# Folding the attention weights of layer 1 at the end of layer 0, and reading them back from DRAM

## The chip, the cores and the metric

The kernel is one program on one core of a Trainium2 chip. The metric is device time in microseconds (us). Times of whole runs are given as a median of several; a profiled execution has its own time, and within it the span from the first instruction to the last.

## What is computed

Two layers run one after the other on x of shape 4 x 512 x 512, all in float32. Layer 0 is a test-time-training scan (32 heads of 16, 32 steps of 16 tokens) beside a gated feed-forward network of width 1408. Layer 1 is a latent attention (16 heads of 128, four batches of 512 tokens here seen as 4 x 512 rows) beside four experts of width 512. Cut to what matters:

```python
xn = layernorm(x)
x = x + ttt_scan(xn) @ o_w.T + ffn(xn)                 # layer 0
xn = layernorm(x)
c_kv = xn @ W_DKV + b_DKV                              # latents, 128 wide
c_q  = xn @ W_DQ + b_DQ                                # latents, 384 wide
k = (c_kv @ W_UK + b_UK).reshape(b, s, H, D)           # H = 16, D = 128
v = (c_kv @ W_UV + b_UV).reshape(b, s, H, D)
q = (c_q @ W_UQ + b_UQ).reshape(b, s, H, D)
q[..., :64] = rope(q @ W_QR); k[..., :64] = rope(k @ W_KR)
probs = softmax(q . k / sqrt(D))
x = x + (probs @ v).reshape(b, s, H * D) @ W_O + b_O + experts(xn)   # layer 1
```

Two products of weights alone can be taken ahead of the tokens. The rotated half of a key or query is c @ (W_U @ W_R), so W_U @ W_R (64 columns per head) is one folded weight; and probs @ v @ W_O is (probs @ c_kv) @ (W_UV @ W_O), so W_UV @ W_O (512 columns per head) is another. What b_UV adds to the output is one row, b_UV @ W_O, which goes into the output bias.

## The kernel before, in words

The program has three stages, each with its own pools.

**Layer 0** (lines 89 to 799). The scan runs 32 steps in eight chunks of four. A step is a chain of small operations over all engines. Between its parts `fill(us)` takes pieces of other work out of one generator, `work`, until the costs that the pieces yield (an estimate of TensorE time) cover the gap: `GAPS` for the steps of chunks 0 to 6, `LAST_GAPS` for those of chunk 7. `work` is `between(ch)` for each chunk: the feed-forward network of the chunk (`gate_up`, `down`), the next chunk's keys, values and queries, the end of the chunk before (`finish`), and in chunks 1 to 4 `value_bias`, which puts b_UV @ W_O of one group of four heads into `bo` by matmuls. `between(7)` also computes the latents c_kv and c_q of chunks 0 to 6 (`latents`) and puts them into DRAM (`lat_d`). After the last step, lines 794 to 799 take `finish(7)` apart by `LAST_FINISH`, then drain `work`, the rest of `finish(7)` and `latents(7)`.

**Experts** (lines 821 to 922). Four experts, each 8 groups of four matmuls 128x512 for gate and up (line 855) and 16 for down (line 900). Their loads go out on SyncE's queue (`fetch`, line 831), but for the first gate weight and 14 parts of the input, which go out on GpSimd's.

**Attention** (lines 928 to 1112). 64 units (group of four heads, batch, head). Each unit has queries and keys (lines 992, 999), scores (1008), softmax (1010 to 1015), probabilities turned by VectorE in 32x32 blocks (1023) and 16 DMAs from SBUF to SBUF (1046), context (1054); after four heads the output (1069). `group_weights` prepares a group: for group 0 ahead of the units, for groups 1 to 3 at the second batch of the group before. It loads W_UK, W_UQ, W_UV and W_O of the group, turns 128x128 blocks by TensorE (937) and ScalarE (939), and multiplies: 16 products of 64 columns (955, copied at 956) and four of 512 (970, copied at 971).

The order of the instructions on each engine is fixed when the program is built, by a scheduler, and each engine runs its own in that order; a DMA is issued by an engine's queue, in order too. The scratch tiles of layer 0 rotate by tag: `wg` and `wu` two buffers each, `wd` four, `sg` and `xr` two each. A tile of a later stage that lies where an earlier one lay waits for the last use of that one.

Of the kernel before, what the change touches and what calls it, by code (L numbers as in the profile page):

```python
# [12 lines left out]
F32 = mybir.dt.float32  # L13
AF = mybir.ActivationFunctionType
ALU = mybir.AluOpType
AX = mybir.AxisListType
PSUM = bass.MemoryType.PSUM

P = 128
B, L, HS = 4, 512, 512  # L20
NT = B * L
NC = HS // P
# [8 lines left out]
NCHUNK = NM // CH  # L31
CW = B * CT
# [1 line left out]
RW = 2 * 64 + 4  # L34

START = 20.0
GAPS, LAST_GAPS = (11.0, 4.0, 8.0), (10.0, 4.0, 5.0)
LAST_FINISH = (9.0, 17.0, 5.0)
TTT_EPS = 1e-6
LN_EPS = 1e-5  # L40

# [3 lines left out]
H, D, KVC, QC, RD = 16, 128, 128, 384, 64  # L45
HALF = RD // 2
THETA = 10000.0
NHG = 4
HPG = H // NHG
# [6 lines left out]
def trunk_kernel(ctx: ExitStack, tc: tile.TileContext, a: dict, out: bass.AP):  # L56
    nc = tc.nc
# [8 lines left out]
    ident = const.tile([P, P], F32, tag="ident", name="ident")  # L66
# [3 lines left out]
    dram = ctx.enter_context(tc.tile_pool(name="dram", bufs=1, space=bass.MemoryType.DRAM))  # L70
    yd = dram.tile([B, L, HS], F32, tag="yd", name="yd")
    xe_d = dram.tile([2 * NCHUNK, P, NC, E, 32], F32, tag="xe_d", name="xe_d")
    lat_d = dram.tile([1 + QC // P, P, B, NCHUNK, CT], F32, tag="lat_d", name="lat_d")
    bo = const.tile([P, HS], F32, tag="bo", name="bo")
    eps_ttt = const.tile([P, 1], F32, tag="eps_ttt", name="eps_ttt")
# [13 lines left out]
    with ExitStack() as px:  # L89
        one = px.enter_context(tc.tile_pool(name="b_one", bufs=1))  # L90
        wk = px.enter_context(tc.tile_pool(name="b_wk", bufs=2))
        ps_pj = px.enter_context(tc.tile_pool(name="b_pspj", bufs=2, space=PSUM))
# [4 lines left out]
        quarters = [slice(32 * q, 32 * q + 32) for q in range(4)]  # L97

        def mm(out, lhsT, rhs, start=True, stop=True):
            nc.tensor.matmul(out, lhsT=lhsT, rhs=rhs, start=start, stop=stop, skip_group_check=True)  # L100

        def psum():
            return ps_pj.tile([P, 512], F32, tag="pj", name="pj")
# [55 lines left out]
        for name in ("gamma", "beta"):  # L159
            nc.scalar.dma_start(  # L160
                out=row[name].rearrange("o (be al x) -> o be al x", be=NC, al=4),
                in_=by_head(name).rearrange("al be h d -> be al (h d)").unsqueeze(0),
# [349 lines left out]
            yield 3.43  # L512


        ones32 = one.tile([P, P], F32, tag="ones32", name="ones32")
        nc.vector.memset(ones32, 1.0 / 32)
        buv16 = one.tile([H, D], F32, tag="buv16", name="buv16")
        nc.gpsimd.dma_start(out=buv16, in_=a["b_UV"].rearrange("(h d) -> h d", d=D))
        buv_b = one.tile([P, H, 32], F32, tag="buv_b", name="buv_b")
        nc.gpsimd.dma_start(out=bo, in_=a["b_O"].unsqueeze(0).to_broadcast([P, HS]))  # L520

        def value_bias(hg):
            if hg == 0:
                pt = psum()[:, :H]
                nc.tensor.transpose(pt, buv16, ident[:H, :H])
                nc.vector.tensor_copy(buv_b, pt.unsqueeze(2).to_broadcast([P, H, 32]))
            pb = psum()
            for h, r in enumerate(quarters):
                w = wk.tile([P, HS], F32, tag="wd", name=f"wob_{hg}_{h}", bufs=4)
                nc.sync.dma_start(out=w, in_=a["W_O"][(4 * hg + h) * D : (4 * hg + h + 1) * D, :])  # L530
                mm(pb[r], buv_b[:, 4 * hg + h, :], w)
            part = wk.tile([P, HS], F32, tag="xt", name=f"bo_part{hg}", bufs=4)
            nc.vector.tensor_copy(part, pb)
            yield 1.3
            pb = psum()
            mm(pb, ones32, part)
            nc.vector.tensor_add(bo, pb, bo)
            yield 0.86

        def over_blocks(t, z):  # L540

# [108 lines left out]
        def between(ch):  # L650

            fin = finish(ch - 1) if ch > 0 else iter(())
            if ch + 1 == NCHUNK:
                latent_operands()
            for i in range(NI):
                yield from gate_up(ch, i)
                if ch + 1 == NCHUNK and i in (2, 5, 8):
                    latent_rows(i // 3)
                if i == NI - 3:
                    yield from take(fin, 1)  # L660
            if ch == 0:
                yield from finish_constants()
            extra = value_bias(ch - 1) if 1 <= ch <= NHG else iter(())
            nxt = iter(())
            if ch + 1 < NCHUNK:
                nxt = chain(
                    norm_turn(ch + 1), keys(ch + 1), token_tile(ch + 1, 0), token_tile(ch + 1, 1), queries(ch + 1)
                )
            else:
                yield from fin  # L670
            for u in range(2):
                dn = down(ch, u)
                for j in range(3):
                    yield from take(nxt, 2)
                    yield from take(dn, 1)
                    yield from take(fin, 1)
            yield from extra
            yield from nxt
            done.add(ch + 1)
            yield from fin  # L680
            if ch + 2 < NCHUNK:
                norm_rows(ch + 2)
            if ch + 1 == NCHUNK:
                for key in sorted(parts, key=str):
                    yield from latents(key)

        def take(it, k):
            for _ in range(k):
# [29 lines left out]
        pt = psum()[:, :P]  # L718
# [76 lines left out]
        for us in LAST_FINISH:  # L795
            fill(us)
            next(fin)
        for _ in chain(work, fin, latents(NCHUNK - 1)):
            pass


# [19 lines left out]
    with ExitStack() as px:  # L821
        one = px.enter_context(tc.tile_pool(name="d_one", bufs=1, reuse_waits="tile"))
        wk = px.enter_context(tc.tile_pool(name="d_wk", bufs=2, reuse_waits="tile"))
        wg = px.enter_context(tc.tile_pool(name="d_wg", bufs=1, reuse_waits="tile"))
        psp = px.enter_context(tc.tile_pool(name="d_ps", bufs=2, space=PSUM))
        gate_w = [one.tile([P, NC, 2 * EI], F32, tag="gu1", name="gu_1")]
        gate_w.insert(0, wg.tile([P, NC, 2 * EI], F32, tag="gu0", name="gu_0"))

# [40 lines left out]
        for e in range(E):  # L869
# [15 lines left out]
                    nc.sync.dma_start(out=cq[:, i], in_=lat_d[1 + i].rearrange("p b k x -> p b (k x)"))  # L885
            inter = wk.tile([P, EI // P, B * P], F32, tag="inter", name=f"inter_{e}")
            for i in range(EI // P):
                pg = psp.tile([P, B * P], F32, tag="pg", name=f"epg_{e}_{i}")
                product(e, pg, gu, i * P)
                pu = psp.tile([P, B * P], F32, tag="pu", name=f"epu_{e}_{i}")  # L890
                product(e, pu, gu, EI + i * P)
                sg = wk.tile([P, B * P], F32, tag="sg", name=f"esg_{e}_{i}")
                nc.scalar.activation(sg, pg, AF.Silu)
                nc.vector.tensor_mul(
                    by_batch(inter[:, i].rearrange("p (b j) -> p b j", b=B)), by_chunk(pu), by_chunk(sg)
                )
# [31 lines left out]
    with ExitStack() as px:  # L928
# [1 line left out]
        ps_pj = px.enter_context(tc.tile_pool(name="e_pspj", bufs=4, space=PSUM))  # L930
        ps_sc = px.enter_context(tc.tile_pool(name="e_pssc", bufs=4, space=PSUM))

        def turned(w, nm):

            pt = ps_pj.tile([P, HPG, P], F32, tag="pj", name=f"ptw_{nm}")
            for h in range(HPG):
                nc.tensor.transpose(pt[:, h, :], w[:, h, :], ident)
            t = wk.tile([P, HPG, P], F32, tag="wt", name=f"wt_{nm}")
            nc.scalar.copy(t, pt)
            return t  # L940

        def group_weights(hg):

            c = slice(hg * HPG * D, (hg + 1) * HPG * D)

            def loaded(name, src, bufs=2):
                t = wk.tile([P, HPG, src.shape[-1] // HPG], F32, tag=name, name=f"{name}_{hg}", bufs=bufs)
                nc.sync.dma_start(out=t, in_=src.rearrange("p (h d) -> p h d", h=HPG))
                return t

            def fold(w, wr, nm):
                wt = turned(w, f"{nm}_{hg}")
                pw = ps_pj.tile([P, HPG, RD], F32, tag="pj", name=f"pw_{nm}_{hg}")
                for h in range(HPG):
                    nc.tensor.matmul(pw[:, h, :], lhsT=wt[:, h, :], rhs=wr, start=True, stop=True)
                nc.scalar.copy(w[:, :, RD:], pw)

            uk = loaded("uk", a["W_UK"][:, c])
            uq = [loaded(f"uq{i}", a["W_UQ"][i * P : (i + 1) * P, c]) for i in range(QC // P)]
            uv = loaded("uv", a["W_UV"][:, c], bufs=1)  # L960
            ow = wk.tile([P, HPG, HS], F32, tag="ow", name=f"ow_{hg}", bufs=1)
            nc.sync.dma_start(out=ow, in_=a["W_O"][c, :].rearrange("(h p) o -> p h o", p=P))
            fold(uk, wkr, "uk")
            for i in range(QC // P):
                fold(uq[i], wqr, f"uq{i}")
            uvt = turned(uv, f"uv_{hg}")
            vo = wk.tile([P, HPG, HS], F32, tag="vo", name=f"vo_{hg}")
            for h in range(HPG):
                pv = ps_pj.tile([P, HS], F32, tag="pj", name=f"pvo_{hg}_{h}")
                nc.tensor.matmul(pv, lhsT=uvt[:, h, :], rhs=ow[:, h, :], start=True, stop=True)  # L970
                nc.scalar.copy(vo[:, h, :], pv)
            return dict(uk=uk, uq=uq, vo=vo)

        def rotate(t, ps, bias, trig, nm):
# [235 lines left out]
```

## Time and profile before

| what | us |
|---|---|
| median of 3 runs (lowest, highest) | 2159.91 (2157.66, 2160.46) |
| the profiled execution, whole | 2162.4 |
| its span | 2160.6 |
| first expert matmul (line 855) | 1022.40 after the start |
| first key matmul of the attention (line 992) | 1209.58 after the start |

| engine | busy us | share of the span | instructions |
|---|---|---|---|
| TensorE (PE) | 2068.6 | 96% | 10050 |
| its weight loads (PEld) | 1181.5 | 55% | 10050 |
| VectorE (DVE) | 1177.5 | 54% | 2384 |
| ScalarE (ACT) | 883.3 | 41% | 1805 |
| GpSimd (POOL) | 504.9 | 23% | 555 |

Times in the profile are us from the span's start unless marked ns. A float32 matmul of the program is two MATMUL records. SPq is SyncE's queue, whose rows are DMA issues: their durations are the time that the issue held the queue, not the transfer.

### The profile page before, as it was taken

Reading aid. Unit: us, or ns where it says so; the run is one execution under the profiler, and the core shown is the slowest. Engines: PE = TensorE matmul, PEld = TensorE weight load, DVE = VectorE, ACT = ScalarE, POOL = GpSimd, SP = SyncE. Lnnn points to the kernel's source line nnn. Section 1 sums busy time; section 2 is a strip of 40 time slices with the busy share of each in tenths; the row PEclk is TensorE's granted clock in tenths of the full one; section 3 lists DMA queues with packets and bytes.
Section 4 is the critical chain, followed back from the end, with each engine's and each line's share of the span. In section 5 each row is a group of like instructions: output and inputs, shape, how many; then the busy total and the mean of one; then the engine's idle time right before and its main releaser. Section 6 shows DMA issues by size and latency. Waiting matters only on the chain.

```text
span 2160.6 us, 29279 instructions
## 1 busy us (share of the span) xinstructions
PE 2068.6 (96%) x10050; PEld 1181.5 (55%) x10050; DVE 1177.5 (54%) x2384; ACT 883.3 (41%) x1805; POOL 504.9 (23%) x555
## 2 busy tenths in 40 slices
PE   8999999999999999995999899999999999999998
PEld 6776676767676767543444444444444444444444
DVE  4445656465656565631111556664666656666663
ACT  2334353434434343332000454444544545455552
POOL 4233233233333333301001211110111111111110
PEclk9999999999999999998999989999999999999999
DMA  6556364646474646526610233333233333333332
GB/s 179 153 138 190 112 193 134 180 135 175 131 197 129 173 136 192 171 75 235 226 59 25 89 92 77 74 94 75 76 77 93 75 72 78 75 75 75 95 94 76
DMA packets 286960, 259.27 MB, mean 120 GB/s; under 512 B 52956, under 2 KB 210845, under 8 KB 285789
## 3 DMA queue, kind: packets, MB, share of 16 engines
q1 hardware_dynamic: 272752, 245.96, 41.0%
q10 hardware_dynamic: 11500, 5.32, 0.9%
q0 software_dynamic: 2560, 6.13, 0.8%
q8 instruction: 81, 1.33, 0.3%
q14 instruction: 67, 0.54, 0.1%
HBM read 161.60 MB, written 29.62 MB: 89 GB/s over the span
## 4 chain that ended last, share of the span: by engine, by line
PE 75%; DVE 10%; ACT 9%; DMA 3%; issue 2%; POOL 1%; SPq 0%; ACTq 0%; DVEq 0%; POOLq 0%
PE pj L100 14%; PE pf L100 11%; PE po L1069 10%; PE pc L1054 7%; PE sc L1008 5%; PE pq L999 5%; PE pd L100 5%; ACT prob L1013 3%; PE epg L855 3%; PE epo L900 3%; PE epu L855 3%; ACT prob L1015 2%; PE pso L100 2%; PE pk L992 2%; PE pz L100 2%
## 5 line engine op out<-in xcount | busy, mean ns | idle before, releaser
L1008 PE MATMUL sc<-kT,qT 96*128 96x512 f32 x512 | 235.7, 598 | 15.1 <-ACT prob L1013 13.5
L985 POOL TENSOR_TENSOR kT<-t_k,t_k 32x512 f32<-32x512 f32 x64 | 80.7, 1261 | 717.9 <-PE pq L999 403.3
L1013 ACT ACTIVATE prob<-sc,mx 128x512 f32<-128x512 f32 x256 | 173.1, 683 | 147.1 <-DVE mx L1010 147.1
L1069 PE MATMUL po<-vo,ctxT 128*128 128x512 f32 x512 | 223.0, 593 | 1.5 <-ACT ctxT L1059 1.5
L1054 PE MATMUL pc<-prT,lv 128*128 128x512 f32 x496 | 224.0, 594 | 0.0
L1023 DVE STREAM_TRANSPOSE tt<-prob 128x512 f32<-128x512 f32 x252 | 166.6, 697 | 60.3 <-ACT prob L1015 56.7
L100 PE MATMUL pf<-xT,wg 128*128 128x256 f32 x704 | 171.8, 385 | 4.2 <-DVE hid L459 3.9
L999 PE MATMUL pq<-cq,uq 128*128 128x512 f32 x384 | 175.2, 592 | 0.0
L1015 ACT ACTIVATE prob<-prob,sm 128x512 f32<-128x512 f32 x256 | 171.7, 724 | 3.6 <-DVE sm L1014 3.6
L1008 PEld LDWEIGHTS sc<-kT,qT 96*128 96x128 f32 x512 | 96.0, 191 | 140.9 <-issue 110.6
L100 PE MATMUL pf<-xT,wu 128*128 128x256 f32 x704 | 168.0, 380 | 0.5 <-DMA wu<-in_wu 0.3
L1010 DVE TENSOR_REDUCE mx<-sc 128x1 f32<-128x512 f32 x256 | 164.4, 681 | 7.0 <-PE sc L1008 4.4
L100 PE MATMUL pd<-wd,hid 128*128 128x512 f32 x352 | 165.2, 600 | 0.2
L1069 PEld LDWEIGHTS po<-vo,ctxT 128*128 128x128 f32 x512 | 97.1, 190 | 124.1 <-issue 116.2
L1054 PEld LDWEIGHTS pc<-prT,lv 128*128 128x128 f32 x496 | 94.5, 191 | 120.0 <-issue 112.1
L100 PEld LDWEIGHTS pf<-xT,wg 128*128 128x128 f32 x704 | 131.0, 190 | 32.1 <-DVE hid L459 6.7
L100 PEld LDWEIGHTS pf<-xT,wu 128*128 128x128 f32 x704 | 133.2, 190 | 22.1 <-issue 2.6
L1079 DVE TENSOR_TENSOR y<-po,y 128x512 f32<-128x512 f32 x64 | 44.2, 691 | 152.5 <-PE po L1069 152.5
L993 ACT ACTIVATE kT<-pk,b_UK 64x512 f32<-64x512 f32 x64 | 43.7, 683 | 196.7 <-PE pk L992 196.7
L999 PEld LDWEIGHTS pq<-cq,uq 128*128 128x128 f32 x384 | 73.0, 190 | 91.8 <-issue 86.8
L459 DVE SCALAR_TENSOR_TENSOR hid<-pf,us,sg 128x256 f32<-128x256 f32 x88 | 41.5, 474 | 132.6 <-ACT sg L458 132.0
L297 POOL TENSOR_SCALAR sk<-k,m 128x256 f32<-128x256 f32 x64 | 61.3, 969 | 158.1 <-PE pz L100 158.1
(256 smaller groups left out, 3151.8 us busy)
## 6 DMA issues: line engine op xcount, KB each, us to landing
prT<-tt SPq DMA_DIRECT2D x1008, 64.0 KB, 2.0
wd<-in_wd SPq DMA_DIRECT2D x176, 256.0 KB, 3.0
wg<-in_wg SPq DMA_DIRECT2D x88, 256.0 KB, 3.5
wu<-in_wu SPq DMA_DIRECT2D x88, 256.0 KB, 3.4
rows<-rows SPq DMA_DIRECT2D x128, 66.0 KB, 2.2
kv<-rows SPq DMA_DIRECT2D x32, 264.0 KB, 4.4
gu<-in_gu SPq DMA_DIRECT2D x3, 2048.0 KB, 8.7
xt<-in_x SPq DMA_DIRECT2D x32, 128.0 KB, 3.2
```

The costliest lines, as they stand in the source:

```text
L100: nc.tensor.matmul(out, lhsT=lhsT, rhs=rhs, start=start, stop=stop, skip_group_check=True)
L855: nc.tensor.matmul(ps, lhsT=w[:, c, col : col + P], rhs=xe[:, :, c, e, :], start=(c == 0), stop=(c == NC - 1))
L900: nc.tensor.matmul(po, lhsT=inter[:, i, b * P : (b + 1) * P], rhs=dn[:, i, :], start=(i == 0), stop=(i == EI // P - 1),)
L985: nc.gpsimd.tensor_sub(t[RD:mid, :], t1[RD:mid, :], t2[RD:mid, :])
L999: nc.tensor.matmul(pq, lhsT=w["uq"][i][:, h, :], rhs=cq[:, i, b, :], start=(i == 0), stop=(i == nq - 1))
L1008: nc.tensor.matmul(ps, lhsT=qT[:KQ, i * P : (i + 1) * P], rhs=kT[:KQ, :], start=True, stop=True)
L1010: nc.vector.tensor_reduce(mx, ps, AX.X, ALU.max, negate=True)
L1013: nc.scalar.activation(pr, ps, AF.Exp, bias=mx, scale=1.0, accum_out=sm)
L1015: nc.scalar.mul(pr, pr, sm)
L1023: nc.vector.transpose(out=tt[:, :, :, i, :], in_=pr.rearrange("p (kb e j) -> p kb e j", e=2, j=K))
L1054: ins = nc.tensor.matmul(pc, lhsT=lv[:, b, k, :], rhs=prT[:, k, :], start=(k == 0), stop=(k == E - 1))
L1069: ins = nc.tensor.matmul(po[e], lhsT=ctxT[:, h, e * P : (e + 1) * P], rhs=w["vo"][:, h, :], start=(h == 0), stop=(h == HPG - 1),)
```

## The change

`value_bias` goes. A new generator `fold(hg)` is put at the end of `between(7)`, after the latents of chunks 0 to 6, for all four groups. For each of five weights of a group (W_UK, three of W_UQ, W_UV) `weights_turned` loads a 128x512 block by 16 DMAs on SyncE's queue, each of 32 x 4 x 32 elements, so that 32x32 blocks land turned as blocks, and one VectorE transpose turns each within itself. The products are those of `group_weights`; ScalarE copies them and its queue stores them in DRAM (`rot_d`, `vo_d`). W_O is loaded by head, and VectorE sums b_UV times its rows into `bo_part`; one matmul adds the partitions into `bo`. `group_weights` now only loads: the unrotated 64 columns of each head, the folded 64, and `vo`. `LAST_GAPS` and `LAST_FINISH` change, the last lines of layer 0 run `latents(7)` ahead of what is left of `work`, and the experts' gate and up PSUM tiles get a pool of their own.

```diff
-GAPS, LAST_GAPS = (11.0, 4.0, 8.0), (10.0, 4.0, 5.0)
-LAST_FINISH = (9.0, 17.0, 5.0)
+GAPS, LAST_GAPS = (11.0, 4.0, 8.0), (11.0, 4.0, 8.0)
+LAST_FINISH = (9.0, 13.0, 6.0, 0.0, 3.0, 0.0)
...
+        def weights_turned(src, nm):
+
+            raw = wk.tile([P, NC, P], F32, tag="wg", name=f"raw_{nm}")
+            view = src.rearrange("(cq r) (h dq d) -> dq r h cq d", r=32, h=HPG, dq=4)
+            for dq, r in enumerate(quarters):
+                for h in range(HPG):
+                    nc.sync.dma_start(
+                        out=raw[r, h].rearrange("r (cq d) -> r cq d", cq=4), in_=view[dq, :, h]
+                    )
+            t = wk.tile([P, HPG, P], F32, tag="wu", name=f"wt_{nm}")
+            nc.vector.transpose(out=t.rearrange("p h c -> p (h c)"), in_=raw.rearrange("p h c -> p (h c)"))
+            return t
+
+        def fold(hg):
+            c = slice(hg * HPG * D, (hg + 1) * HPG * D)
             if hg == 0:
                 pt = psum()[:, :H]
                 nc.tensor.transpose(pt, buv16, ident[:H, :H])
...
+                nc.vector.tensor_copy(buv, pt)
+            ups = [a["W_UK"][:, c]] + [a["W_UQ"][i * P : (i + 1) * P, c] for i in range(QC // P)]
+            for i, src in enumerate(ups):
+                wt = weights_turned(src, f"{hg}_{i}")
+                pw = psum()[:, : HPG * RD].rearrange("p (h d) -> p h d", h=HPG)
+                for h in range(HPG):
+                    mm(pw[:, h, :], wt[:, h, :], wr2[:, min(i, 1)])
+                st = wk.tile([P, CW], F32, tag="sg", name=f"rot_{hg}_{i}")
+                nc.scalar.copy(st, pw.rearrange("p h d -> p (h d)"))
+                nc.scalar.dma_start(out=rot_d[hg, i], in_=st.rearrange("p (h d) -> p h d", h=HPG))
+                yield 1.3
+            wt = weights_turned(a["W_UV"][:, c], f"{hg}_v")
+            for h in range(HPG):
+                hh = hg * HPG + h
+                ow = wk.tile([P, HS], F32, tag="wd", name=f"ow_{hh}", bufs=4)
+                nc.sync.dma_start(out=ow, in_=a["W_O"][hh * D : (hh + 1) * D, :])
+                pv = psum()
+                mm(pv, wt[:, h, :], ow)
+                st = wk.tile([P, HS], F32, tag="xr", name=f"vo_{hh}")
+                nc.scalar.copy(st, pv)
+                nc.scalar.dma_start(out=vo_d[hg, :, h], in_=st)
...
+                    nc.vector.scalar_tensor_tensor(bo_part, ow, buv[:, hh : hh + 1], bo_part, ALU.mult, ALU.add)
+                yield 0.9
+            if hg == NHG - 1:
+                pb = psum()
+                mm(pb, onesd, bo_part)
+                nc.vector.scalar_tensor_tensor(bo, pb, float(HS), bo, ALU.mult, ALU.add)
+                yield 0.86
...
-            extra = value_bias(ch - 1) if 1 <= ch <= NHG else iter(())
...
-            yield from extra
...
                 for key in sorted(parts, key=str):
                     yield from latents(key)
+                for hg in range(NHG):
+                    yield from fold(hg)
...
-        for _ in chain(work, fin, latents(NCHUNK - 1)):
+        for _ in chain(latents(NCHUNK - 1), work):
             pass
...
+        ps_gu = px.enter_context(tc.tile_pool(name="d_psgu", bufs=2, space=PSUM))
...
-                pg = psp.tile([P, B * P], F32, tag="pg", name=f"epg_{e}_{i}")
+                pg = ps_gu.tile([P, B * P], F32, tag="pg", name=f"epg_{e}_{i}")
...
-            def loaded(name, src, bufs=2):
-                t = wk.tile([P, HPG, src.shape[-1] // HPG], F32, tag=name, name=f"{name}_{hg}", bufs=bufs)
-                nc.sync.dma_start(out=t, in_=src.rearrange("p (h d) -> p h d", h=HPG))
+            def loaded(name, src, i):
+                t = wk.tile([P, HPG, D], F32, tag=name, name=f"{name}_{hg}")
+                nc.sync.dma_start(out=t[:, :, :RD], in_=src[:, c].rearrange("p (h d) -> p h d", h=HPG)[:, :, :RD])
+                nc.sync.dma_start(out=t[:, :, RD:], in_=rot_d[hg, i])
                 return t
...
+            uk = loaded("uk", a["W_UK"], 0)
+            uq = [loaded(f"uq{i}", a["W_UQ"][i * P : (i + 1) * P], 1 + i) for i in range(QC // P)]
             vo = wk.tile([P, HPG, HS], F32, tag="vo", name=f"vo_{hg}")
...
+            nc.sync.dma_start(out=vo, in_=vo_d[hg])
             return dict(uk=uk, uq=uq, vo=vo)
```

More of the change, by code (lines that the diff above doesn't have):

```diff
@@ L72, in trunk_kernel @@
     xe_d = dram.tile([2 * NCHUNK, P, NC, E, 32], F32, tag="xe_d", name="xe_d")
+    rot_d = dram.tile([NHG, 1 + QC // P, P, HPG, RD], F32, tag="rot_d", name="rot_d")
+    vo_d = dram.tile([NHG, P, HPG, HS], F32, tag="vo_d", name="vo_d")
     lat_d = dram.tile([1 + QC // P, P, B, NCHUNK, CT], F32, tag="lat_d", name="lat_d")
@@ L512, in finish_constants @@
             yield 3.43
-        ones32 = one.tile([P, P], F32, tag="ones32", name="ones32")
-        nc.vector.memset(ones32, 1.0 / 32)
+        wr2 = one.tile([P, 2, RD], F32, tag="wr2", name="wr2")
+        nc.gpsimd.dma_start(out=wr2[:, 0], in_=a["W_KR"])
+        nc.gpsimd.dma_start(out=wr2[:, 1], in_=a["W_QR"])
         buv16 = one.tile([H, D], F32, tag="buv16", name="buv16")
         nc.gpsimd.dma_start(out=buv16, in_=a["b_UV"].rearrange("(h d) -> h d", d=D))
-        buv_b = one.tile([P, H, 32], F32, tag="buv_b", name="buv_b")
+        buv = one.tile([P, H], F32, tag="buv", name="buv")
+        bo_part = one.tile([P, HS], F32, tag="bo_part", name="bo_part")
         nc.gpsimd.dma_start(out=bo, in_=a["b_O"].unsqueeze(0).to_broadcast([P, HS]))
-        def value_bias(hg):
+        def weights_turned(src, nm):
[11 more added lines that the diff above has]
+            c = slice(hg * HPG * D, (hg + 1) * HPG * D)
             if hg == 0:
@@ L525, in value_bias @@
                 nc.tensor.transpose(pt, buv16, ident[:H, :H])
[L526 to L538, printed above, removed]
+                nc.vector.tensor_copy(buv, pt)
[9 more added lines that the diff above has]
+                yield 1.3
@@ new lines, in fold @@
+            wt = weights_turned(a["W_UV"][:, c], f"{hg}_v")
[8 more added lines that the diff above has]
+                nc.scalar.dma_start(out=vo_d[hg, :, h], in_=st)
+                if hh == 0:
+                    nc.vector.tensor_scalar_mul(bo_part, ow, buv[:, :1])
+                else:
+                    nc.vector.scalar_tensor_tensor(bo_part, ow, buv[:, hh : hh + 1], bo_part, ALU.mult, ALU.add)
+                yield 0.9
@@ L887, in trunk_kernel @@
             for i in range(EI // P):
-                pg = psp.tile([P, B * P], F32, tag="pg", name=f"epg_{e}_{i}")
+                pg = ps_gu.tile([P, B * P], F32, tag="pg", name=f"epg_{e}_{i}")
                 product(e, pg, gu, i * P)
-                pu = psp.tile([P, B * P], F32, tag="pu", name=f"epu_{e}_{i}")
+                pu = ps_gu.tile([P, B * P], F32, tag="pu", name=f"epu_{e}_{i}")
                 product(e, pu, gu, EI + i * P)
@@ L931, in trunk_kernel @@
         ps_sc = px.enter_context(tc.tile_pool(name="e_pssc", bufs=4, space=PSUM))
[L933 to L940, printed above, removed]
         def group_weights(hg):
             c = slice(hg * HPG * D, (hg + 1) * HPG * D)
-            def loaded(name, src, bufs=2):
-                t = wk.tile([P, HPG, src.shape[-1] // HPG], F32, tag=name, name=f"{name}_{hg}", bufs=bufs)
-                nc.sync.dma_start(out=t, in_=src.rearrange("p (h d) -> p h d", h=HPG))
-                return t
[L951 to L966, printed above, removed]
@@ L967, in group_weights @@
+            def loaded(name, src, i):
+                t = wk.tile([P, HPG, D], F32, tag=name, name=f"{name}_{hg}")
+                nc.sync.dma_start(out=t[:, :, :RD], in_=src[:, c].rearrange("p (h d) -> p h d", h=HPG)[:, :, :RD])
+                nc.sync.dma_start(out=t[:, :, RD:], in_=rot_d[hg, i])
+                return t
+            uk = loaded("uk", a["W_UK"], 0)
+            uq = [loaded(f"uq{i}", a["W_UQ"][i * P : (i + 1) * P], 1 + i) for i in range(QC // P)]
             vo = wk.tile([P, HPG, HS], F32, tag="vo", name=f"vo_{hg}")
[L968 to L971, printed above, removed]
+            nc.sync.dma_start(out=vo, in_=vo_d[hg])
```

## The prediction

> **What bounds the kernel now.** I read the rows of slices first, then TensorE's order of work around the two places that the change touches, then SyncE's queue there. In the slices TensorE is the bound, layer 0 and attention alike:
>
> ```profile
> PE   8999999999999999995999899999999999999998
> DVE  4445656465656565631111556664666656666663
> PEclk9999999999999999998999989999999999999999
> DMA  6556364646474646526610233333233333333332
> ```
>
> A slice is 54 us. The one hole is slice 19 (972 to 1026 us), the passage from the scan to the experts. So work taken from TensorE in attention is time saved, and work added in layer 0 is time lost, unless it fits in that hole. The timeline of TensorE shows the hole and what precedes it:
>
> ```profile
> 945.63 0.68 PE L100 MATMUL pso<-a_bd,gh 128*32 128x68 f32 x32
> 946.25 7.13 PE L100 MATMUL pj<-xl,W_DQ 128*128 128x512 f32 x16
> ...
> 981.26 0.59 PE L100 MATMUL pj<-pn_sq,onesd 128*128 128x256 f32 x2
> 993.57 0.98 PE L100 MATMUL pj<-onesd,pn_sq 128*128 128x1 f32 x4 [11.71 <-DVE pn_sq L543]
> ...
> 1022.40 5.88 PE L855 MATMUL epg<-xe,gu 128*128 128x512 f32 x8 [6.74 <-ACT lat L637]
> ```
>
> The scan's last product is at 945.63, the first expert at 1022.40; between them TensorE waits some 22 us (11.71, 6.74 and smaller). SyncE's timeline of the same stretch:
>
> ```profile
> 946.83 3.01 SPq L437 DMA_DIRECT2D z<-zch  x4
> 952.16 0.38 SPq L439 DMA_DIRECT2D zb<-z  x1
> 1008.61 2.47 SPq L831 DMA_DIRECT2D xe<-xe_d  x2
> ```
>
> The last step's result leaves at 946.83, and the queue is empty until 1008.6. That empty stretch is where the change puts its loads.
>
> **Saved in attention.** The group weights vanish from TensorE and ScalarE. The timeline brackets them: group 2, for one, starts and ends with
>
> ```profile
> 1486.42 0.60 PE L937 MATMUL ptw_uk<-ident,uk 128*128 128x128 f32 x4
> ...
> 1498.87 3.70 PE L970 MATMUL pvo<-ow,wt_uv 128*128 128x512 f32 x8 [0.67 <-ACT wt_uv L939]
> 1502.40 1.02 PE L992 MATMUL pk<-ckv,uk 128*128 128x512 f32 x2
> ```
>
> 1502.40 - 1486.42 = 16.0 us, less 8 score records in between (two rows of 1.72 between starts) = 12.5. Group 3 likewise 1737.76 - 1721.78 - 3.44 = 12.5. Group 1 runs at a granted clock of 0.73: 1267.05 - 1247.83 - 1.72 = 17.5. Group 0 stands alone between the last expert product (ends 1191.9) and the first key (1209.58): 17.7. Sum **60 us**. In the start of attention ScalarE may be next in line (scores wait 4.00 us for it at 1239.98), so I allow 45 to 65. The loads that replace these (nine DMAs a group for six, four extra of 64 columns) go before they are needed, since two buffers exist; SyncE's 16 prT issues of 0.64 us take 10.2 of 13.7 us of a unit, so there is room.
>
> **Saved in layer 0.** `value_bias` is 16 + 4 matmuls of 512 columns, 0.86 us each by their rows: **17 us** on a TensorE that is 97 to 99% busy in chunks 1 to 4. Its VectorE and DMA work was beside this.
>
> **Moved across the scan's end.** With the longer gaps the instruction order has nearly all the latents of chunks 0 to 6 before the last `pso`, where before 29.2 us of them came after (7.13 + 3.60 + 3.60 + 3.70 + 3.70 + 1.89 + 5.60). 5.6 us stay behind. So the scan ends 23.6 us later.
>
> **The new loads, the step that decides.** 20 weights x 16 = 320 issues on SyncE, plus 16 of W_O; the 16 W_O loads of `value_bias` go, but they lay in chunks 1 to 4. The instruction order puts 64 of the 320 before the last step's z store, 256 behind it, and all of them ahead of the experts' loads. TensorE's order is as strict: the first products of `finish(7)` stand behind seven folded weights, its mean behind fifteen, its transposes and `latents(7)` behind group 3's. So the path to the first expert runs through the whole queue. No row shows this load. The nearest is the attention's turn, the same shape of destination, 32 rows by 4:
>
> ```profile
> L1046 SPq DMA_DIRECT2D prT<-tt x1008: 585/599/1982, 1227.7 to 2137.0; - x168
> L277 SPq DMA_DIRECT2D rows<-rows x128: 303/430/1938, 31.2 to 827.5; - x128
> L454 SPq DMA_DIRECT2D wg<-in_wg x88: 327/328/727, 14.5 to 869.5; - x88
> ```
>
> Minimum, median and maximum are in ns. Back to back, ten prT issues took 6.39 us, 0.64 each. Lower end: the wg row at 0.33 plus 0.04 between, 0.37. Upper end: about 1.0, if eight loads in flight (the program rotates eight completion semaphores on this queue) land as slowly as trig_k's 64-byte pieces do in the tile's rows, up to 7.4 us. I take **0.64**, because shape and queue agree. Behind z:
>
> - z store, then W_UV's first load waits for VectorE to turn an earlier weight, and VectorE for TensorE's 5.6 us of latents and the first fold: 9 us, with `finish(7)`'s own load (zb) and all further weights queued behind it;
> - 256 x 0.64 = 164 us;
> - 12 W_O loads at 0.43 (the kind's unspaced issues): 5 us;
> - from there landing, turn, product, transposes and `latents(7)`, of which the same stretch took 1022.4 - 1003.9 = 18.5 us before, plus some 5 for the last fold: 24 us. The first gate weight (GpSimd's queue) waits on a fold tile too, and needs about as long (977.63 to 996 before), so it lies beside.
>
> Sum 202 us, against 1022.4 - 946.8 = 75.6 before. The fold's own TensorE work (16 weights' products of 0.83 to 1.1 us, 16 of 0.86, one more: about 31 us), VectorE's 20 turns and 16 sums at about 0.7, ScalarE's 32 copies (0.37 and 0.59) and stores (0.52 an issue, as lat_d's) all lie under 10.2 us of issue per weight and cost nothing; if issue were free they would be the cost.
>
> The 64 early issues take 41 us of a queue that also carries `wd` in chunk 7. Four buffers of `wd` cover about 3.4 us, while one block of 15 issues holds the queue 9.6 us. Between nothing and 41 us; most finds idle SyncE time (872.8 to 885.1 is empty before), so I take 7.
>
> **The sum.** Scan's end: 946.8 - 17 + 23.6 + 7 = about 961 to 962. First expert: 962 + 202 = 1164, 142 us later than 1022.4. The experts keep their length. The PSUM pool removes the wait on ScalarE at 1022, but the order of TensorE has the last folds there instead. Attention gives back 60. Net **+81 us** on the profiled execution's 2162.4, so 2243.8; that execution is 2.5 above the median of the runs shown, which gives **2241**.
>
> **Two rules against the rows.** The Trainium skill, "DMA: Bandwidth & Descriptors", section "Issuing engines are not separate DMA queues", says that the sequencer's time to start a DMA is usually small beside the DMA. By that rule the queue is free, the fold costs TensorE's 31 us, of which the 22 us of idle hide most, and the sum is 2162 - 17 + 31 - 22 - 60, about 2094. By the prT row a weight costs 10.2 us for 256 KB; the row decides here. The same page's table of specifications asks for pieces of at least 512 bytes for line rate, and these are of 128. By the rule the transfers themselves might be slow; the trace's DMA records show the few 128-byte packets at 13 ns median, so 128 of them over 16 engines are about 0.1 us, below the issue. This rule adds nothing to the sum.
>
> **Rivals.**
>
> - *Cheaper issue.* The loads take the rows' and W_O's 0.43 + 0.04 = 0.47: 256 x 0.17 = 43.5 us less, **2197**. For it: prT is the slowest form of its size on the queue, and has SBUF on both sides. Against: 64-row loads from DRAM (xt) show 0.594 as well. Chance 0.20.
> - *Early stalls or slow landing.* The 64 early issues hold back `wd` and the last step's stores fully: 34 us more, **2275**; slow landings would go beyond 2300. Chance 0.12.
> - *Faster after all.* One mechanism: the queue does not set the pace of the stretch between z and the experts, and TensorE does. Price: down to 2094. It decides below a spacing of 0.64 - 81/256 = 0.32 us per issue. For it: single rows stores fell to 0.303. Against: nothing back to back is below 0.42, and even spaced wg issues are 0.327. Chance 0.07.
> - No change: the chance of landing within 0.2% (4 us, about what a measurement of this kernel can tell) is 0.01.
>
> The forecast case has 0.60, its own range 2215 to 2265. The range 2180 to 2285 takes in the cheaper issue and most of the stalls, and leaves about 0.15 outside. Faster 0.07, same 0.01, slower 0.92.
>
> **What would show it.** After: the raw loads' issues near 0.6 us and without gaps from the z store to the experts' loads; TensorE mostly idle for about 150 us there, a hole of three slices; the first expert near 1164; no L937-like rows in attention, and attention shorter by 45 to 65. Wrong would be: issues of 0.3 us; TensorE busy in the stretch; or z held up by far more than 15 us.

## The result, and the profile after

| | before | after |
|---|---|---|
| median of the runs on one chip, us | 2160.18 (2157.66 to 2165.19, 4 runs) | 2299.38 (2296.53 to 2300.26, 4 runs) |
| profiled execution: whole / span, us | 2162.4 / 2160.6 | 2300.3 / 2298.4 |
| mean granted TensorE clock | 0.987 | 0.952 |

The changed kernel takes 1.064 times as long (95% interval 1.062 to 1.066): 139 us more. The direction was as predicted; the size (2241) and the range (up to 2285) were not. TensorE's row of slices, its granted clock and the DMA row of the profile after:

```profile
PE   8999999999999989963539998999999999999999
PEclk9999999999999999985669998999999999999999
DMA  6555555555555546433483123233433333333332
```

A slice is now 57 us. The one slice with a hole has become four, 17 to 20 (977 to 1207 us, the digits 6353), with a clock of 0.5 to 0.6 in three of them. The 8 of the DMA row in slice 20 is a burst that will matter below. TensorE's timeline of the passage (start, duration, line, operation, and in brackets the idle time ahead of it and what ended it):

```profile
994.44 0.68 PE L102 MATMUL pso<-a_bd,gh 128*32 128x68 f32 x32
...
1025.26 1.94 PE L102 MATMUL pj<-wr,wt 128*128 128x64 f32 x8 [2.41 <-DVE wt L537]
1032.74 1.94 PE L102 MATMUL pj<-wr,wt 128*128 128x64 f32 x8 [5.54 <-DVE wt L537]
...
1162.40 1.12 PE L102 MATMUL pj<-bo_part,onesd 128*128 128x512 f32 x2
1201.70 5.76 PE L893 MATMUL epg<-xe,gu 128*128 128x512 f32 x8 [38.18 <-DMA xe<-xe_d]
...
1371.90 1.12 PE L1005 MATMUL pk<-ckv,uk 128*128 128x512 f32 x2 [0.78 <-DVE y L945]
```

These instants and the same ones of before split the whole difference:

| stretch | before | after | difference | forecast |
|---|---|---|---|---|
| start to the scan's last `pso` | 945.6 | 994.4 | +48.8 | +15 |
| last `pso` to the first expert | 76.8 | 207.3 | +130.5 | +126 |
| first expert to the first key | 187.2 | 170.2 | -17.0 | -17.7 |
| first key to the end of the span | 951.0 | 926.5 | -24.5 | -42.5 |
| sum | 2160.6 | 2298.4 | +137.8 | +81 |

The second row looks like a hit, but is one by two errors that cancel: the queue took less than forecast, and what comes behind it more. SyncE's timeline shows the first part:

```profile
995.64 5.03 SPq L439 DMA_DIRECT2D z<-zch  x4
1002.83 2.88 SPq L533 DMA_DIRECT2D raw_v<-in_W_UV  x4
1005.87 0.39 SPq L441 DMA_DIRECT2D zb<-z  x1
...
1014.24 7.54 SPq L533 DMA_DIRECT2D raw<-in_W_UK  x16
1021.88 24.66 SPq L533 DMA_DIRECT2D raw<-in_W_UQ  x48
...
1142.52 1.80 SPq L560 DMA_DIRECT2D ow<-in_W_O  x4
1162.53 0.80 SPq L869 DMA_DIRECT2D xe<-xe_d  x2
```

From z's store to the last `ow` load (1144.3) the queue issues almost without a gap: 149 us. 48 loads in a row take 24.66 us, 0.51 each, and 16 take 7.54, 0.47 each; over all 256 loads behind z the mean is 0.52 (the slowest blocks of 16 take 9.55 us). The loads' own row, minimum, median and maximum of an issue in ns:

```profile
L533 SPq DMA_DIRECT2D raw<-in_W_UQ x192: 311/430/1445, 912.0 to 1132.5; - x192
```

The second part is the 57 us from 1144.3 to the first expert, where 24 were forecast. Of these TensorE waits 38.18 for `xe`. GpSimd's timeline tells when the experts' first load goes out, in the kernel before (under the latents) and in the changed one (behind everything):

```profile
977.63 0.83 POOL L844 DMA_DIRECT2D gu<-in_gu  x1
...
1162.77 0.84 POOL L882 DMA_DIRECT2D gu<-in_gu  x1 [113.00 <-DMA lat_d<-lat]
```

### The profile page after: what moved, and what is told of

The parts are those of the page before. It is cut to its first block, busy times and chain, and to the rows that moved or that the text cites. A ratio compares the mean times of both kernels' runs of the same rounds, so it can differ in the third digit from the quotient of the medians.

```text
span 2298.4 us, 29595 instructions
## 1 busy us (share of the span) xinstructions
PE 2082.8 (91%) x9932; PEld 1190.6 (52%) x9932; DVE 1194.6 (52%) x2412; ACT 876.2 (38%) x1787; POOL 504.3 (22%) x557
## 4 chain that ended last, share of the span: by engine, by line
PE 63%; DVE 13%; ACT 9%; DMA 5%; issue 4%; SPq 3%; POOL 2%; DVEq 0%; ACTq 0%; POOLq 0%
PE pj L102 14%; PE pf L102 10%; PE po L1082 10%; PE pc L1067 5%; PE pq L1012 4%; PE sc L1021 4%; ACT prob L1026 4%; PE pd L102 4%; ACT prob L1028 3%; SPq L533 3%; PE epg L893 3%; PE epo L938 2%; PE epu L893 2%; PE pz L102 1%; DMA xe<-xe_d 1%
## 5 line engine op out<-in xcount | busy, mean ns | idle before, releaser
L1021 PE MATMUL sc<-kT,qT 96*128 96x512 f32 x512 | 244.0, 615 | 23.3 <-ACT prob L1026 12.1
L102 PE MATMUL pf<-xT,wg 128*128 128x256 f32 x704 | 180.0, 398 | 18.7 <-DVE hid L461 18.7
L102 PEld LDWEIGHTS pf<-xT,wg 128*128 128x128 f32 x704 | 136.1, 198 | 50.7 <-DVE hid L461 21.8
## 6 DMA issues: line engine op xcount, KB each, us to landing
gu<-in_gu SPq DMA_DIRECT2D x3, 2048.0 KB, 17.7
```

What stands on the lines that cost most here:

```text
L1021: nc.tensor.matmul(ps, lhsT=qT[:KQ, i * P : (i + 1) * P], rhs=kT[:KQ, :], start=True, stop=True)
```

## The experiments

Three questions stand: why the scan is 49 us longer, whether the issues set the pace behind it, and what the 38 us are. Twelve kernels were run, two of them (the bias by sums one at a time, and group 0 alone in the hole) also to find a better version. Ratios are against runs of the kernel before on the same chip, whose median lay between 2161 and 2163 in every set.

**Without value_bias.** From the kernel before, the smallest part of the change alone: the sums over W_O's rows are left out.

```diff
-            extra = value_bias(ch - 1) if 1 <= ch <= NHG else iter(())
+            extra = iter(())
```

> The kernel before without value_bias (the row b_UV @ W_O is left out of the output bias) and nothing else changed. Theory: taking value_bias out removes 17 us of TensorE work but locks scan and feed-forward in a repeating order with more stalls, so the scan's last product comes near 970 us instead of 945.6, chunks 2 to 6 each take 116 us as in the changed kernel, and the time is about 2175 to 2185. Rival (the early loads and the longer last gaps are the whole cause of the later scan end): the last product comes near 929 us and the time falls by about 17 us to 2143.

2184.01 us, ratio 1.0106 (1.0088 to 1.0123). Work that TensorE no longer does makes the kernel 22 us slower. The last `pso` comes at 972.88 instead of 945.63. The main waits of TensorE from 175 to 943 us (total us, times, longest), first of the kernel before, then of the changed kernel:

```profile
PE pj L100 <- DVE pn_sq L543: 7.9, 8, 1.9
PE pso L100 <- POOL gh L404: 4.2, 3, 2.5
PE pf L100 <- DVE hid L459: 1.6, 2, 1.0
...
PE pf L102 <- DVE hid L461: 15.7, 5, 3.1
PE pj L102 <- DVE pn_sq L580: 12.7, 8, 1.9
PE pj L102 <- ACT pn_sq L587: 6.5, 7, 2.4
PE pso L102 <- POOL gh L406: 5.8, 1, 5.8
```

This run, which has nothing else of the change, shows the changed kernel's list again: 15.7, 12.4, 6.5 and 5.8 us.

**One load for a weight.** From the changed kernel; the blocks then stand elsewhere, so the folded weights are others, with the same number of instructions on the compute engines.

```diff
-            view = src.rearrange("(cq r) (h dq d) -> dq r h cq d", r=32, h=HPG, dq=4)
-            for dq, r in enumerate(quarters):
-                for h in range(HPG):
-                    nc.sync.dma_start(
...
+            nc.sync.dma_start(out=raw.rearrange("p h c -> p (h c)"), in_=src)
```

> The changed kernel with each weight block loaded as it lies by one DMA instead of 16 (the 32x32 blocks then stand in the wrong places, so the folded weights are not the right ones); all else stays. Theory (issue time of the loads on SyncE's queue sets the stretch from the z store to the last W_O load, 148 us): the stretch falls to about 50 to 60 us, set by TensorE and by the end of the scan's last chunk, and the time falls by about 90 to 2210. Rival (each weight's chain of landing, turn, product, copy and store sets the pace): the stretch stays above 110 us and the time above 2260.

2215.1 us, ratio 1.025 (1.0233 to 1.0268): 84 us less than the changed kernel. From z to the last raw load are now 58 us, and the fold's last product comes at 1072.77 instead of 1162.40. The edit also makes the pieces of a load longer (2 KB instead of 128 bytes); the next run leaves them as they are.

**Half of the issues on GpSimd's queue.**

```diff
-                    nc.sync.dma_start(
+                    (nc.gpsimd if h % 2 else nc.sync).dma_start(
```

> The changed kernel with every second one of the 16 loads of a weight on GpSimd's queue. Issue theory: the 256 issues behind the z store halve to 128 on each queue, 0.47 us each on SyncE and about 0.54 on GpSimd, so the stretch falls from 148 to 75 to 85 us and the time to about 2230 to 2240. Rival (landing or the DMA engines set the pace): the stretch stays above 130 us, the time above 2280.

2249.68 us, ratio 1.041 (1.0392 to 1.0428): 50 us less, with the same loads and the same bytes. From z to the last `ow` load are now 93 us. That is somewhat more than was expected; GpSimd's queue stands still for some 9 us between its issues, mostly until earlier loads land. With the run before, this shows that the issues, and not the transfers or the fold's work, set the pace of that stretch in the changed kernel. Two queues would also relieve a limit on loads in flight, but there a load landed 1.9 us after its issue in the median, in less time than four issues take.

**The next stage's loads.** In both of these runs the wait for `xe` stays what it was, 38.56 and 38.73 us. From 1163 to 1202 us the changed kernel moves 15.0 MB, 384 GB/s in the mean, with all DMA engines busy. First trial: `y` behind `xe`, on GpSimd's queue.

```diff
-            fetch(out=y[b], in_=rows_of(yd, b))
+            tc.keep_in_program_order(nc.gpsimd.dma_start(out=y[b], in_=rows_of(yd, b)))
```

> The changed kernel with the four loads of y (4 MB) on GpSimd's queue behind the experts' input, instead of on SyncE's beside it. Theory (from the fold's end to the first expert the DMA engines are the bound, and 4 of some 14 MB are not needed yet): TensorE's wait for xe falls from 38.2 to about 27 to 30 us, the time by 8 to 11 us to about 2290. Rival (the first gate weight and the input alone need the time, because GpSimd's queue is slow): no change, 2299.

2302.07 us, ratio 1.0648 (1.0625 to 1.067): nothing gained. But the input itself came earlier: the last part of `xe` landed at 1192.5 (issued at 1183.38, landed 9.1 us later) and not at 1201.4 (1189.11 and 12.3) as in the changed kernel. What ate the gain was TensorE's order, which had changed: two small products now stand ahead of the first expert, and the first of them waits for the load of `b_UK`, which runs beside all the others:

```profile
1203.08 0.36 PE L951 MATMUL pb<-b_UK,W_KR 128*64 128x16 f32 x2 [41.04 <-DMA b_UK<-in_b_UK]
...
1203.94 5.69 PE L893 MATMUL epg<-xe,gu 128*128 128x512 f32 x8
```

Second trial: the second expert's `gu` and `dn` behind `y` as well.

```diff
-            fetch(out=gu, in_=a["gu"][e].rearrange("(c p) o -> p c o", p=P))
+            fetch(nc.gpsimd if e == 1 else nc.sync, out=gu, in_=a["gu"][e].rearrange("(c p) o -> p c o", p=P))
...
-            fetch(out=dn, in_=a["dn"][e].rearrange("(c p) o -> p c o", p=P))
+            fetch(nc.gpsimd if e == 1 else nc.sync, out=dn, in_=a["dn"][e].rearrange("(c p) o -> p c o", p=P))
```

> The changed kernel, with y and the second expert's gu_1 and dn_1 on POOL's queue behind xe. Theory: TensorE's 38 us before the first expert are the time that some 15 MB of loads need at 400 GB/s, all let go at 1162; with only gu_0, xe and dn_0 (7.3 MB) ahead, the first expert starts at about 1185 instead of 1202 and the whole is 2282 to 2290. Rival: xe itself sets the time by its own queue, whatever else is loaded: 1202 and 2299.

2304.67 us, ratio 1.0664 (1.065 to 1.0679). No gain again, and for the same kind of reason: the last part of `xe` landed at 1185.4, but the edit let later loads move up, and with them TensorE's order changed. The timeline of this run:

```profile
1159.91 1.12 PE L102 MATMUL pj<-bo_part,onesd 128*128 128x512 f32 x2
...
1206.55 3.58 PE L959 MATMUL lv_tr<-ident,ckv 128*128 128x128 f32 x16 [25.86 <-DMA ckv<-lat_d]
1209.96 2.31 PE L893 MATMUL epg<-xe,gu 128*128 128x512 f32 x5
```

A transpose of `ckv` now stands ahead of the first expert and waits for its own load. Third trial, with these loads kept in place too, and TensorE's order that of the changed kernel:

```diff
-                nc.sync.dma_start(out=wqr, in_=a["W_QR"])
...
-                nc.sync.dma_start(out=ckv, in_=lat_d[0].rearrange("p b k x -> p b (k x)"))
+                fetch(nc.gpsimd, out=wqr, in_=a["W_QR"])
...
+                fetch(nc.gpsimd, out=ckv, in_=lat_d[0].rearrange("p b k x -> p b (k x)"))
```

> As the run e7_next_loads_behind, whose first expert stood behind a product that waited for ckv: here the loads of the second expert's step (W_QR to cq) also keep their place on POOL's queue, so that TensorE's order is that of the changed kernel. Theory: the 38 us before the first expert are bytes, and with 7 MB instead of 15 MB ahead of xe's last tile the first expert starts at 1183 to 1190 and the whole is 2282 to 2290. Rival: the bytes behind xe don't matter, or what is spared here is paid by the second expert that waits for gu_1: 2299.

2281.23 us, ratio 1.0547 (1.0532 to 1.0562): 18 us less than the changed kernel, as the bytes would have it.

```profile
1183.74 6.56 PE L893 MATMUL epg<-xe,gu 128*128 128x512 f32 x8 [22.84 <-DMA xe<-xe_d]
```

The wait falls from 38.18 to 22.84 us, and no new wait comes up among the experts. So 15 of the 38 us are the time of bytes that the first expert does not need. That the other 23 are bytes too is read from the trace and not tried: from 1160 to 1184 us this run moves 8.7 MB at 361 GB/s.

**The pauses.** value_bias gave the planner two values, 1.3 and 0.86, in each of four chunks. They are put back with no instruction behind them, once in the changed kernel and once in the kernel before without its sums.

```diff
+            extra = iter((1.3, 0.86)) if 1 <= ch <= NHG else iter(())
...
+            yield from extra
             yield from nxt
```

> The changed kernel, with the two pauses that value_bias gave back to the planner (1.3 and 0.86, in chunks 1 to 4) kept, and no instruction behind them: the same work in another order. Theory: the scan is longer in the changed kernel because without these two steps the planner deals the filling work out differently, in a worse pattern that repeats in every chunk; with the pauses back the last pso comes some 15 to 40 us earlier than 994 and the whole is 2260 to 2285. Rival: the scan is longer because of the work that was moved into it or the early loads, not because of the pattern: 2299, last pso at 994.

> The kernel before without value_bias (its sums over W_O's rows are left out), the two pauses kept. Theory (pattern): the order of before comes back, and the sums' own 17 us of TensorE are saved: 2143 to 2152, last pso at about 930. Rival (the pauses don't set the order, or these gaps are filled by something else): 2184, as without the pauses.

2243.83 us (ratio 1.0389, 1.0373 to 1.0405) and 2144.89 us (0.9937, 0.9924 to 0.9951). Nothing is computed or loaded that was not before, and 56 and 39 us are gone. In the first that is more than was expected, in the second as much. TensorE's waits from 175 to 943 us in the first of them, to be set beside the list above:

```profile
PE pj L102 <- DVE pn_sq L580: 7.4, 7, 1.9
PE pz L102 <- ACT wq_bd L317: 4.9, 5, 1.0
PE pf L102 <- DVE hid L461: 2.4, 3, 1.0
```

The last `pso` comes at 943.25 instead of 994.44. In the second run it comes at 926.13, 19.5 us ahead of the kernel before (5 of them stand already at the end of chunk 0, ahead of the first removed product; the whole is 16 us shorter). So the products of value_bias were worth about the 17 us of TensorE that were forecast, but its 2.16 us of planner's time per chunk held an order in place whose loss costs far more. From 175 us to the last `pso` TensorE sits idle for 44.9 us in the changed kernel and for 21.1 us with the pauses: 24 of the 51 us. The other 27 are recorded as busy time. 7 of these are latents that come ahead of the last `pso` (72 `W_DQ` matmuls of 512 columns instead of 56). Another part goes with the mean granted clock, 0.98 instead of 1.00 with the pauses: the `pf<-xT,wg` products, the first behind a wait for `hid`, take 401 ns in the mean instead of 383, the `pf<-xT,wu` products of the same shape 381 instead of 379. How the rest divides, and why the order without the pauses waits more, was not settled.

**The bias by sums, alone.** From the kernel before: sums on VectorE at the old place, with the old pauses.

```diff
-                mm(pb[r], buv_b[:, 4 * hg + h, :], w)
...
+                    nc.vector.scalar_tensor_tensor(bo_part, w, buv[:, hh : hh + 1], bo_part, ALU.mult, ALU.add)
```

> The kernel before with only the third part of the change: values' bias by sums on VectorE (16 W_O loads, one scalar_tensor_tensor each, one last matmul), at the old places and with the old pauses. Theory: TensorE is spared some 16 us of value_bias, and VectorE has room for 4 sums in a chunk: 2143 to 2155. Rival: VectorE's sums come late and hold TensorE as much as the products did: 2160 or more.

2175.07 us, ratio 1.0072 (1.0059 to 1.0084): the rival. The list of waits of this run has a new first line:

```profile
PE pso L100 <- POOL gh L404: 16.4, 4, 5.8
```

The sums, 0.75 us each, stand close together on VectorE among the scan's own work (three without a gap at 260.48, four between 494.1 and 498.2), and within 11 us behind each of the four groups TensorE waits once for `gh`. So the next kernel puts one sum behind each of gate_up's steps 1, 3, 5 and 7.

```diff
                 yield from gate_up(ch, i)
+                if 1 <= ch <= NHG and i in (1, 3, 5, 7):
+                    value_bias(HPG * (ch - 1) + i // 2)
```

> As the run e8_bias_sums_paced, but the 16 sums one at a time, behind gate_up's steps 1, 3, 5 and 7 of chunks 1 to 4, instead of four in a row. Theory: those four (0.75 us each, 3 us together) stood ahead of the scan's own work on VectorE, and TensorE waited 16 us for gh; one at a time they fit into VectorE's waits, and the kernel takes what the run without the sums took, 2145 to 2153. Rival: VectorE has no room for 12 us more, wherever they stand: 2165 to 2180.

2157.06 us, ratio 0.9974 (0.9964 to 0.9983), with 2.1 us of waits for `gh`. That is between the two forecasts: a third of the 17 us is gained, and the last `pso` at 937.6 is still 11 us behind the run without any sums. Of these 11 us, 8 stand already at the end of chunk 0 (`zch` at 178.2, against 170.3): 4 came before the first sum (158.7), for a reason that was not found, and 4 in the step in which the first four sums stand. From there to the end of chunk 4, behind the last sum, it is 1.6 us more. So VectorE has room for most of them. The scheduler did not spread them all, though: three of the second group still stand without a gap at 280.60, and TensorE does not wait for `gh` there. It is the place of the sums that counts, and not only how many stand in a row.

**Group 0 alone, in the hole.** On top of that kernel, group 0's weights are folded at the end of layer 0, with plain loads and TensorE's transposes, and parked in DRAM; groups 1 to 3 stay where they were.

```diff
-LAST_FINISH = (9.0, 17.0, 5.0)
+LAST_FINISH = (9.0, 17.0, 12.0)
...
                 for key in sorted(parts, key=str):
                     yield from latents(key)
+                yield from fold0()
```

> As e10_bias_sums_spread, and group 0's weights alone folded at the end of the first layer (plain loads, blocks turned by TensorE as before), in the 20 us in which TensorE waits for the last chunk's norm, and parked in DRAM. Theory: the expert stage becomes 17 us shorter, as it did in the changed kernel, and the fold lies in a hole: 8 to 15 us less than e10_bias_sums_spread, about 2135 to 2142. Rival: the fold's tiles hold back gu_0 and xe, as in the changed kernel, and the first expert comes 10 to 20 us later: 2145 to 2160.

2148.62 us, ratio 0.9938 (0.9923 to 0.9952), 8 us less than without it. First expert to first key falls from 191.4 to 169.7 us; the passage to the experts grows from 77.7 to 94.1, more than was hoped. The fold's first products stand ahead of the last chunk's mean, which comes 6 us later behind the last `pso` than without them:

```profile
979.65 1.97 PE L102 MATMUL pj<-wr,wt 128*128 128x64 f32 x8 [1.48 <-ACT wt L554]
981.41 1.17 PE L102 MATMUL pj<-pn_sq,onesd 128*128 128x256 f32 x2
```

Another 9 us pass between these two products of the mean and its next ones (21 us, against 12), with the rest of the fold and 5.17 us of waiting for ScalarE's copy of its result. The time lies in the rival's range, and the fold does hold `gu_0` back (issued at 990.74, against 969.75), but TensorE's wait ahead of the first expert is for the latents (5.69 us), not for a load. It is 0.6% faster than the kernel before.

**Both cures in the changed kernel.** The pauses and one load for a weight.

> The changed kernel with both cures: the two pauses kept, and one plain load for a weight instead of 16 (the blocks stand elsewhere, so the folded weights are others). Theory: the two losses are independent, 55 us and 84 us, and add up: 2299 - 55 - 84 = 2160, between 2150 and 2170, the time of before. Rival: one hides the other (both are waits on the same queue): 2190 or more.

2177.56 us, ratio 1.0075 (1.0057 to 1.0094): 122 us less than the changed kernel, where the parts sum to 140. Nearly, but not wholly independent. The last `pso` is at 942.22 and the first expert at 1073.99: the passage takes 131.8 us, 55 more than in the kernel before, and attention with the experts gives 40 back. Of the 55 us, about 25 lie ahead of TensorE's last product of layer 0, with the fold; the rest is the wait of the first expert for `xe`, 36.21 us, where the kernel before waited 6.74 for the latents.

## Why the prediction was wrong

Against the forecast, the scan's end is 34 us worse, the queue 29 better, what comes behind the queue 33 worse, and attention gives 18 less: together the 57 by which the span was missed.

- **value_bias, -17.** The size was about right where the order is kept, the conclusion was not: the step priced the removed products and not the removed yields. Taking both away reorders all that follows them; alone it moved the scan's end by +27 us where -17 were forecast, and giving the pauses back gave 51 us there. **This is the step that failed first.** The instruction order was read for where the latents and loads went, and not for what happens in chunks 2 to 7. Chunks 2 to 5 of the changed kernel took 116.1 us each, alike to a tenth: a pattern that repeats. In the kernel before they took 97 to 126, 111 in the mean.
- **Latents moved, +23.6, and early stalls, +7.** With the pauses in both, the changed kernel's scan ends 17.1 us after that of the kernel without sums (943.25 and 926.13). Forecast: 30.6. Fewer latents moved than was read from the order: 14 us of their matmuls of 512 columns more stand ahead of the last `pso` (36.2 us, against 21.9). And the early loads stalled little: TensorE waits 2 us more (21.1 and 19.0).
- **The issues, 0.64 us each.** The mechanism holds: one load instead of 16 gives 84 us, a second queue 50. The size was 0.52 in the mean, nearer to the rival with cheaper issue (0.47). `prT` was the wrong row; the median of 430 ns is that of `rows`, which are stores to DRAM, while `xt`, loads from DRAM, show 594. What makes an issue dear was not tried. Z to the last load took 149 us where 178 were forecast. This error of -29 hid in the sum.
- **The tail, 24.** It took 57. "The first gate weight needs about as long ... so it lies beside" failed. The 18 us were misread: before, `gu` landed 8.6 us after its issue at 977.63, and what landed at 996 was the last of the 14 parts of `xe` behind it. And nothing of it lies beside: the load goes out at 1162.77, when the trace has the last latents stored, 18.4 us behind the last `ow` load, and there every load of the next stage is let go at once, 15.0 MB, which at 384 GB/s are 39 us. The forecast put this at nothing. In the kernel before, part of the same loads lay beneath the latents from 977.63 on.
- **The experts.** They kept their length, and group 0's 17.7 us came as 17.0.
- **Attention, -60 (45 to 65).** It came to -41.5, just outside. Counted from the first key, the changed kernel's key products are 1.2 us ahead just before group 2's weights, 12.8 just before group 3's, and 24.7 later on. So groups 2 and 3 gave nearly their 12.5 us each, and of group 1's 17.5 there is 1. The start of attention in the changed kernel shows whom TensorE waits for instead:

```profile
1395.31 5.40 PE L1021 MATMUL sc<-kT,qT 96*128 96x512 f32 x8 [1.97 <-POOL qT L998]
1403.01 2.88 PE L1021 MATMUL sc<-kT,qT 96*128 96x512 f32 x4 [2.30 <-ACT prob L1026]
...
1435.99 3.78 PE L1021 MATMUL sc<-kT,qT 96*128 96x512 f32 x4 [4.62 <-POOL qT L998]
```

The waits for GpSimd's `qT` over the first 129 us of attention, after and before:

```profile
PE sc L1021 <- POOL qT L998: 11.1, 5, 4.6
PE sc L1008 <- POOL qT L985: 1.7, 2, 1.4
```

Group 1's fold had stood in their place. The forecast looked for the next in line on ScalarE; it was GpSimd. That is read from the two traces, not tried.

Two sums of the forecast are off by little: 946.8 - 17 + 23.6 + 7 is 960.4 and not 961 to 962, and the waits in TensorE's hole before come to 26 us and not 22 (11.71, 6.74, 2.88, 2.66, 1.19, 0.68, 0.48).

The rivals: *cheaper issue* was near the right duration but not the time, *early stalls* named the right direction for a wrong reason, *faster* and *no change* fell. The rule that starting a DMA is usually small beside the DMA (the Trainium skill, "DMA: Bandwidth & Descriptors", section "Issuing engines are not separate DMA queues") did not help with 16 small loads in a row: 7.5 us of issue at the least for 256 KB, each part landing 1.9 us after its issue in the median. It holds for the one plain load of the same 256 KB: 0.33 us of issue, 3.6 us to landing.

## What to carry to other kernels

A step that is removed from a list which a planner deals out takes its planned time along as well as its work; compare the order of the instructions over all that follows, or keep the pause and take away the work alone. Count DMAs, not bytes, where one queue carries many small ones, and carry the whole range of the rows that can be read beforehand (here 0.33 to 0.64 us; it was 0.52). Before work is put into a hole, ask which of the next stage's loads were being fetched beneath the work around it; here 15.0 MB came late together, and TensorE waited 38 us.

## What the runs showed that was not expected

Less than nine planned microseconds with nothing in them (four times 2.16) were worth 39 and 56 us. The same 16 VectorE sums of 0.75 us cost TensorE 14 us more waiting in one place than in another (16.4 and 2.1 us for `gh`). And to hold back bytes at a busy stage boundary, moving some loads to another queue was twice no use: `xe` landed 9 and 16 us earlier, but another product moved up in TensorE's order and waited for its own load as long.
